# A four-layer decoder: attentions 0 and 3 in whole steps of two chunks, with three banks of scores

## The chip, the cores and the metric

The kernel runs on one core of one Trainium2 chip. The metric is the device time of one launch in microseconds (us), lower being better; the figure that counts is the median of several runs. TensorE is PE in the profile (PEld is its weight load), VectorE is DVE, ScalarE is ACT, GpSimd is POOL, and SyncE (SP) only issues transfers.

## The reference

`x` is (8, 256, 128): eight batches of 256 tokens. A context `ctx_512` is (8, 1601, 64). Four layers follow each other, each a cross-attention of `x` on the context and then a feed-forward block, all with residuals. This change concerns the attentions of layers 0 and 3, which have the same form, 16 heads of 8 channels:

```python
qh = (layernorm(x) @ Wq + bq)   # -> 16 heads x 8 channels, scaled by 8 ** -0.5
kh, vh = ctx @ Wk + bk, ctx @ Wv + bv
attn = softmax(qh @ kh.T)       # (8 batches, 16 heads, 256, 1601)
x = x + (attn @ vh).reshape(8, 256, 128) @ Wo + bo
```

(Layer 3 has no biases.) The attentions of layers 1 and 2 and the four feed-forward blocks are computed by other code.

## The kernel before

Both attentions run through the function `narrow`. The work is cut into 32 **units**: unit `n` is batch `b = n // 4` and a group `i = n % 4` of four heads. The keys and queries of a unit lie in two tiles each (`t` = 0, 1), and each tile holds two heads, one on its partitions 0 to 63 and one on 64 to 127 (`g` = 0, 1). Every value is split into a high and a low half, so a head of 8 channels fills up to 64 rows. The two heads of a tile are multiplied by two matmuls of 64 rows that lie in the two halves of the array and can run side by side.

The 1601 keys are 13 **chunks** of 128 (the last has 65). For each unit there are three kinds of work:

- **Scores** (`score`, L1069): keys stationary, queries moving, so the scores stand transposed, keys on partitions. One call treats a pair of chunks of one tile: four matmuls of 256 columns into two PSUM banks (tile `st`), one bank for each head. ScalarE takes the exponential of each bank (L1072) into the tile `e`, of which there are two in turn; one `e` holds four heads by two chunks.
- **Values** (`values`, L1081): for one chunk, four matmuls of 32 columns side by side, one for each head, accumulated over the chunks in one bank (`ov`). The operands are plain float32 and each matmul is recorded as two passes, so a chunk shows as eight. At a unit's end ScalarE copies the bank out (L1085).
- **Maxima** (`pair`, L873 and L876): the softmax needs each query's largest score beforehand. Two units ahead, the same scores are computed the other way round (queries stationary, 512 keys moving) and VectorE takes the maximum of each bank. A unit has 14 such pairs of matmuls: 12 with 512 keys, and for each tile one with the last 66 keys of both query blocks (four small matmuls). `shift` then puts the maxima together, and `place_shift` (L895) transposes them and writes them into spare rows of the queries by a transfer.

Besides, smaller steps for later batches are spread over the units from a list `beside` with due times between 0 and 1: loads of keys and queries into a ring of four (`place`, POOL's and SP's queues), the projections (`make_q`, `make_k` L777, `make_v` L834, in attention 0 also the transposes of the context L761), the output projection (L913), and in the last units steps of the feed-forward block that follows. All of those that use TensorE take a bank from the same ring as the scores (`bank()`).

The order on every engine is that of the program text (`manual_schedule`). Units take seven **steps** `p` of two chunks (the seventh has one), and each step is two **half steps** `t`. A half step issues the scores of tile `t`, then the values of one chunk of the step before, then what is due of `beside`, then what is due of `tasks`, where the pairs of maxima stand: one for each half step in the steady state, shifted by `DONE` = 8 half steps against the unit. The eight banks are three for the maxima (tag `m`, one bank a buffer), four for scores and side steps (`s`) and one for the values (`o`). A tile is allocated from its ring in turn, and the first matmul into it waits until the last reader of the tile that had the buffer before is done.

Of the kernel before, what the change touches and what calls it, by code (L numbers as in the profile page):

```python
# [33 lines left out]
F32 = mybir.dt.float32  # L34
F32R = mybir.dt.float32r
AF = mybir.ActivationFunctionType
ALU = mybir.AluOpType
AX = mybir.AxisListType

P = 128  # L40
# [9 lines left out]
TAKEN = -3.0e38  # L50
KW = LK + 1
RING = 4
DONE = 8
AFTER = 26


# [1 line left out]
def decoder_kernel(ctx: ExitStack, tc: tile.TileContext, a: dict, out: bass.AP):  # L58
    nc = tc.nc
# [7 lines left out]
    ps = {}  # L67
    big = {}

    @contextmanager  # L70
    def psum(**bufs):
        with ExitStack() as es:
            for n, k in bufs.items():
                ps[n] = es.enter_context(tc.tile_pool(name=f"ps_{n}", bufs=k, space=PS))
            yield
            ps.clear()

    def pm():
        return ps["m"].tile([P, 512], F32, tag="m", name="pm")
# [594 lines left out]
    def narrow(wq, wkT, wvT, wo, bq, bk, bv, bo, first, after=None, last=None):  # L674
# [8 lines left out]
        with ExitStack() as es:  # L683
            one = es.enter_context(tc.tile_pool(name="na1", bufs=1))
            two = es.enter_context(tc.tile_pool(name="na2", bufs=2))
            es.enter_context(psum(m=3, s=4, o=1))
            es.enter_context(tc.manual_schedule())

            def bank():
# [43 lines left out]
            def spare(n):  # L733

                pt = ps["o"].tile([P, LQ], F32, tag="o", name="ov")
                for _ in range(n):
                    nc.tensor.matmul(pt, lhsT=wkh, rhs=K[0][0][:, 0:LQ], start=True, stop=True)
# [124 lines left out]
            def maxima(n):  # L862

                mx = two.tile([P, QT, 4, 4], F32, tag="mx", name="mx", bufs=3)
                last = KW - 1536

                def pair(t, js, at, w):
                    k, q = K[n % RING][t], Q[n % RING][t]
                    pt = [pm() for g in range(2)]
                    for x, j in enumerate(js):  # L870
                        for g in range(2):
                            r = slice(64 * g, 64 * g + 64)
                            nc.tensor.matmul(pt[g][:, x * w:(x + 1) * w], lhsT=q[r, j * P:(j + 1) * P],  # L873
                                             rhs=k[r, at:at + w], start=True, stop=True)
                    for g in range(2):
                        nc.vector.tensor_reduce(mx[:, js[0]:js[-1] + 1, 2 * t + g, at // 512],  # L876
                                                pt[g][:, 0:len(js) * w].rearrange("p (j k) -> p j k", k=w),
                                                AX.X, ALU.max)

                def shift():  # L880
                    m = two.tile([P, QT, 4], F32, tag="mxn", name="mxn")
                    nc.vector.tensor_reduce(m, mx, AX.X, ALU.max, negate=True)
                    mq = M[n % 2].rearrange("p j (h s) -> p j h s", s=8)
                    nc.vector.tensor_copy(mq[:, :, :, 0], m)
                    nc.vector.tensor_tensor(mq[:, :, :, 1], m, mq[:, :, :, 0].bitcast(F32), ALU.subtract)

                order = [(j, at) for at in (0, 512, 1024) for j in range(QT)]
                return [f for t in range(2) for f in
                        (*(lambda j=j, t=t, at=at: pair(t, (j,), at, 512) for j, at in order),
                         lambda t=t: pair(t, range(QT), 1536, last))], shift  # L890
# [130 lines left out]
            for n in range(units):  # L1021
                b, i = divmod(n, 4)
                v = V[b % 2]
                if n + 2 < units:
                    plan(n + 2)

                beside = []
                if n + 3 < units:
                    beside += [((0.0, 0.25)[t], lambda t=t: place(n + 3, t)) for t in range(2)]
                beside.append((0.3, lambda: load_later(3)))  # L1030
                if n + 1 < units:
                    beside.append(((DONE + 1) / per, lambda: place_shift(n + 1)))
                if b + 1 < NB and i == 0:
                    beside += zip((0.0, 0.2, 0.5, 0.65, 0.8, 1.0),
                                  (lambda: turn_y(b + 1), lambda: make_q(b + 1), *make_k(b + 1)))
                if b + 1 < NB and i == 1:
                    beside += zip((0.2, 0.4, 0.6, 0.8), make_v(b + 1))
                if b and i == 2:
                    beside += zip((0.2, 0.35, 0.6), finish(b - 1))
                if b + 2 < NB and i == 2:  # L1040
                    load_ct(b + 2)
                    if first:
                        cuts, turns = make_ct(b + 2)
                        beside += zip((0.0, 0.0, 0.4, 0.6), cuts)
                        beside += zip((0.3, 0.5, 0.7, 0.9), turns)
                if b + 3 < NB and i == 3:
                    beside.append((0.0, lambda: load_raw(b + 3)))
                if b + 2 < NB and i == 3:
                    beside.append((0.5, lambda: (make_y(b + 2), add_bias(b + 2))))
                if after is not None and n >= AFTER:  # L1050
                    if n == AFTER:
                        late = after(left(), bank)
                    beside += [((x - per * (n - AFTER)) / per, lambda x=x: run([late[x]], EARLY + LATE))
                               for x in late if x // per == n - AFTER]
                beside.sort(key=lambda x: x[0])
                if i == 0:
                    od[b] = two.tile([P, LQ], F32, tag="od", name="od")
                    sums[b] = two.tile([P, LQ], F32, tag="sums", name="sums")
                cell = {}

                def score(p, t, e):
                    k, q = K[n % RING][t], Q[n % RING][t]
                    cs = range(2 * p, min(2 * p + 2, NC))
                    m = P if cs[-1] < NC - 1 else LAST
                    st = [bank().rearrange("p (j q) -> p j q", q=LQ) for g in range(2)]
                    for j, c in enumerate(cs):
                        for g in range(2):
                            r = slice(64 * g, 64 * g + 64)
                            nc.tensor.matmul(st[g][0:m, j, :], lhsT=k[r, c * P:c * P + m], rhs=q[r, :],  # L1069
                                             start=True, stop=True)  # L1070
                    for g in range(2):
                        nc.scalar.activation(e[0:m, 2 * t + g, 0:len(cs), :], st[g][0:m, 0:len(cs), :], AF.Exp)  # L1072

                def values(c, e, cell=cell, i=i, v=v, b=b):
                    if c == 0:
                        cell["o"] = ps["o"].tile([P, LQ], F32, tag="o", name="ov")
                    m = P if c < NC - 1 else LAST
                    for g in range(4):
                        h = 4 * i + g
                        at = 2 * D * c + 32 * (h // 2) + 2 * (h % 2)  # L1080
                        nc.tensor.matmul(cell["o"][32 * g:32 * g + 32, :], lhsT=v[0:m, at:at + 32],  # L1081
                                         rhs=e[0:m, g, c % 2, :], start=(c == 0), stop=(c == NC - 1))
                    if c == NC - 1:
                        os = two.tile([P, LQ], F32, tag="os", name="os")
                        nc.scalar.copy(os, cell["o"])  # L1085
                        at = slice(32 * i, 32 * i + 32)
                        nc.sync.dma_start(out=od[b][at, :], in_=os[0:P:4, :])
                        nc.sync.dma_start(out=sums[b][at, :], in_=os[1:P:4, :])

                for p in range(steps):  # L1090
                    e = two.tile([P, 4, 2, LQ], F32, tag="e", name="e")
                    for t in range(2):
                        score(p, t, e)
                        if n == p == 0:
                            spare(6)
                        if before:
                            before.pop(0)()
                        while beside and (beside[0][0] * 2 * steps < 2 * p + t + 1 or p * t == steps - 1):
                            beside.pop(0)[1]()
                        for f in tasks.pop(per * n + 2 * p + t, []):  # L1100
                            f()
                    before = [lambda c=c, e=e, values=values: values(c, e)
                              for c in range(2 * p, min(2 * p + 2, NC))]
            *inverses, project = finish(NB - 1)
# [829 lines left out]
```

## Time and profile before

| what | us |
|---|---|
| median of 3 runs | 3535.34 (3530.77 to 3539.5) |
| the profiled execution: span from first to last instruction | 3529.4 |
| PE busy in the span | 3380.6 (96%) |
| DVE busy | 2580.6 (73%) |
| ACT busy | 2290.0 (65%) |
| first and last scores (L1069) of attention 0, from the span's start | 55.5 to 705.8 |
| first and last scores (L1069) of attention 3 | 2685.9 to 3317.0 |

The page gives the profiled execution's span and not a time of its own beside it; the three times are 1.4 to 10.1 us above the span, the median 5.9. A matmul's recorded duration holds the time in the pipeline, so that a busy PE may still lose time between its groups; start-to-start distances show this better. "pm", "st", "ov" are the PSUM tiles of maxima, scores and values.

### The profile page before, as it was taken

To read this page: it belongs to the slowest core of one execution; us is meant where nothing else is said; L and a number is where in the kernel's file an instruction comes from. 1 tells how busy PE (TensorE), PEld (TensorE's weight loads), DVE (VectorE), ACT (ScalarE), POOL (GpSimd) and SP (SyncE) were. 2 spreads that over 40 slices of the span, in tenths; PEclk is the share of its full clock that TensorE was granted. 3 is DMA by queue.
4 is the path that set the end of the run, shared out by engine and by line. 5 is a ranking of instruction groups with operands and counts; after the bars stand their busy time and mean duration, and the time that the engine had idled before them with its cause. 6 is when DMAs were issued, how large, how long until landed. Compare 5 with 4: busy or idle time off the path is not lost.

```text
span 3529.4 us, 75160 instructions
## 1 busy us (share of the span) xinstructions
PE 3380.6 (96%) x28453; PEld 2299.7 (65%) x28453; DVE 2580.6 (73%) x6482; ACT 2290.0 (65%) x5747; POOL 1179.4 (33%) x2105
## 2 busy tenths in 40 slices
PE   7999999989999999999999999988999999999999
PEld 4555555468787877788787878866445555555444
DVE  6888888656776767676776767675557888888665
ACT  3888887746666666667666666654224878787622
POOL 6344344624152513324151520131115333332100
PEclk8999999989999999999999999999998999999999
DMA  5544444120001001000100000021004444443100
GB/s 97 89 73 74 71 77 58 19 83 1 15 1 33 2 1 39 1 15 1 39 1 22 6 1 15 1 66 33 1 0 85 78 63 68 65 69 53 41 5 7
DMA packets 113449, 130.24 MB, mean 37 GB/s; under 512 B 67616, under 2 KB 96832, under 8 KB 112448
## 3 DMA queue, kind: packets, MB, share of 16 engines
q1 hardware_dynamic: 92352, 114.22, 18.0%
q0 software_dynamic: 20480, 10.53, 1.3%
q8 instruction: 225, 3.69, 0.4%
q10 hardware_dynamic: 256, 0.69, 0.1%
q14 instruction: 136, 1.11, 0.1%
HBM read 44.79 MB, written 11.28 MB: 16 GB/s over the span
## 4 chain that ended last, share of the span: by engine, by line
PE 81%; DVE 9%; ACT 6%; POOL 2%; issue 2%; DMA 0%; DVEq 0%; POOLq 0%; SPq 0%; ACTq 0%
PE ov L1081 13%; PE o L514 12%; PE st L467 12%; PE pm L873 11%; PE t L500 8%; PE st L1069 6%; PE gu L1740 3%; PE o L1789 3%; PE gu L1741 3%; ACT pt L502 3%; DVE ls L474 2%; DVE mx L876 2%; ACT e L488 2%; PE st L834 1%; DVE ql L444 1%
## 5 line engine op out<-in xcount | busy, mean ns | idle before, releaser
L876 DVE TENSOR_REDUCE mx<-pm 128x1 f32<-128x512 f32 (+1 forms) x1792 | 1020.3, 627 | 172.7 <-PE pm L873 168.9
L1072 ACT ACTIVATE e<-st 128x512 f32<-128x512 f32 (+1 forms) x1792 | 910.6, 566 | 210.5 <-PE st L1069 160.0
L474 DVE TENSOR_REDUCE ls<-st 128x1 f32<-128x512 f32 x1088 | 549.5, 567 | 292.3 <-PE st L467 291.2
L488 ACT ACTIVATE e<-st,ls 128x512 f32<-128x512 f32 x1088 | 634.0, 602 | 13.4 <-DVE ls L477 12.6
L502 ACT COPY pt<-t 128x512 f32<-128x512 f32 x544 | 293.6, 586 | 460.8 <-PE t L500 459.9
L1081 PE MATMUL ov<-e,V 128*32 128x256 f32 x6656 | 564.6, 392 | 0.3 <-ACT e L1072 0.3
L873 PE MATMUL pm<-K,Q 64*128 64x512 f32 (+1 forms) x2048 | 497.3, 451 | 18.6 <-DVE mx L876 15.4
L500 PE MATMUL t<-ident,e 128*128 128x128 f32 (+1 forms) x3536 | 506.5, 281 | 2.6
L514 PE MATMUL o<-pt,v 128*64 128x128 f32 (+1 forms) x7072 | 490.2, 278 | 17.0 <-DVE pt L502 13.0
L514 PEld LDWEIGHTS o<-pt,v 128*64 128x64 f32 (+1 forms) x7072 | 412.1, 137 | 88.2 <-DVE pt L502 37.2
L873 PEld LDWEIGHTS pm<-K,Q 64*128 64x128 f32 x2048 | 226.1, 187 | 325.8 <-DVE mx L876 223.3
L500 PEld LDWEIGHTS t<-ident,e 128*128 128x128 f32 (+1 forms) x3536 | 391.5, 141 | 52.4 <-ACT pt L502 30.0
L467 PE MATMUL st<-ct,qh 128*128 128x512 f32 x1088 | 406.1, 373 | 1.8 <-ACT e L488 1.8
L1069 PE MATMUL st<-Q,K 64*128 64x256 f32 (+1 forms) x3328 | 403.1, 287 | 0.1
L467 PE MATMUL st<-ct,ql 128*128 128x512 f32 x1088 | 362.9, 367 | 0.0
L1069 PEld LDWEIGHTS st<-Q,K 64*128 64x128 f32 (+1 forms) x3328 | 333.1, 182 | 32.3 <-issue 6.5
L855 POOL DMA_DIRECT2D Q<-qh x256 | 128.3, 501 | 450.5 <-PE st L1069 422.9
L502 DVE COPY pt<-t 128x512 f32<-128x512 f32 (+1 forms) x544 | 239.1, 481 | 34.9 <-PE t L500 34.8
L467 PEld LDWEIGHTS st<-ct,qh 128*128 128x128 f32 x1088 | 205.6, 189 | 86.3 <-issue 34.9
L1081 PEld LDWEIGHTS ov<-e,V 128*32 128x32 f32 x6656 | 142.5, 108 | 153.7 <-issue 37.9
L1742 ACT ACTIVATE act<-gu 128x512 f32<-128x512 f32 x130 | 77.5, 597 | 243.2 <-PE gu L1741 232.1
L488 ACT ACTIVATION_READ_ACCUMULATOR e<-st,ls 128x1 f32 x1088 | 230.7, 212 | 0.0
(545 smaller groups left out, 4302.2 us busy)
## 6 DMA issues: line engine op xcount, KB each, us to landing
K<-kh SPq DMA_DIRECT2D x250, 100.1 KB
K<-kl SPq DMA_DIRECT2D x250, 100.1 KB
ct<-ctd SPq DMA_DIRECT2D x23, 801.0 KB
ctd<-ct SPq DMA_DIRECT2D x8, 801.0 KB
v<-in_ctx SPq DMA_DIRECT2D x16, 384.0 KB
Q<-qh POOLq DMA_DIRECT2D x256, 16.0 KB, 2.7
Q<-ql POOLq DMA_DIRECT2D x256, 16.0 KB, 3.0
raw<-in_ctx SPq DMA_DIRECT2D x8, 384.0 KB
```

The source lines that it names most:

```text
L467: nc.tensor.matmul(st[n, c][:, 0:w], lhsT=q[k, h][i][:, j * P:(j + 1) * P], rhs=ct[k][:, at:at + w], start=(i == 0), stop=(i == 1))
L474: nc.vector.tensor_reduce(ls[n][:, c:c + 1], st[n, c][:, 0:BANK[c][1]], AX.X, ALU.max)
L488: nc.scalar.activation(e[n][:, at:at + w], st[n, c][:, 0:w], AF.Exp, bias=ls[n][:, 4:5], scale=1.0, accum_out=ls[n][:, 5 + c:6 + c])
L500: nc.tensor.transpose(t[0:m, (c - 4 * i) * P:(c - 4 * i + 1) * P], e[n][:, c * P:c * P + m], ident)
L502: (nc.scalar.copy if i < 2 else nc.vector.tensor_copy)(p[0:m, 0:w], t[0:m, 0:w])
L514: nc.tensor.matmul(o[n][half, 0:P], lhsT=v[k][0:m, c, :], rhs=turned[n, c // 4][0:m, (c % 4) * P:(c % 4 + 1) * P], start=(c < 2), stop=(c ...
L855: nc.gpsimd.dma_start(out=q[r:P:8, :].bitcast(F32), in_=qhl[b][r % 2][src, :].bitcast(F32))
L873: nc.tensor.matmul(pt[g][:, x * w:(x + 1) * w], lhsT=q[r, j * P:(j + 1) * P], rhs=k[r, at:at + w], start=True, stop=True)
L876: nc.vector.tensor_reduce(mx[:, js[0]:js[-1] + 1, 2 * t + g, at // 512], pt[g][:, 0:len(js) * w].rearrange("p (j k) -> p j k", k=w), AX.X, ...
L1069: nc.tensor.matmul(st[g][0:m, j, :], lhsT=k[r, c * P:c * P + m], rhs=q[r, :], start=True, stop=True)
L1072: nc.scalar.activation(e[0:m, 2 * t + g, 0:len(cs), :], st[g][0:m, 0:len(cs), :], AF.Exp)
L1081: nc.tensor.matmul(cell["o"][32 * g:32 * g + 32, :], lhsT=v[0:m, at:at + 32], rhs=e[0:m, g, c % 2, :], start=(c == 0), stop=(c == NC - 1))
```

## The change

In `narrow` alone (both attentions): a pair of maxima is one tile of two banks with one reduction instead of two; the maxima have two such tiles (four banks), scores and side steps have three banks instead of four. A step is no longer two half steps: it issues the scores of tile 0, then the pairs of maxima due in both half steps, then the scores of tile 1, then what is due of `beside`, then the values of both chunks of the step before. `DONE` is 6 instead of 8.

```diff
-DONE = 8
+DONE = 6
...
-            es.enter_context(psum(m=3, s=4, o=1))
+            es.enter_context(psum(mm=2, s=3, o=1))
...
                 def pair(t, js, at, w):
                     k, q = K[n % RING][t], Q[n % RING][t]
-                    pt = [pm() for g in range(2)]
+                    pt = ps["mm"].tile([P, 2, 512], F32, tag="mm", name="pm")
                     for x, j in enumerate(js):
                         for g in range(2):
                             r = slice(64 * g, 64 * g + 64)
-                            nc.tensor.matmul(pt[g][:, x * w:(x + 1) * w], lhsT=q[r, j * P:(j + 1) * P],
+                            nc.tensor.matmul(pt[:, g, x * w:(x + 1) * w], lhsT=q[r, j * P:(j + 1) * P],
                                              rhs=k[r, at:at + w], start=True, stop=True)
-                    for g in range(2):
-                        nc.vector.tensor_reduce(mx[:, js[0]:js[-1] + 1, 2 * t + g, at // 512],
-                                                pt[g][:, 0:len(js) * w].rearrange("p (j k) -> p j k", k=w),
+                    to = mx[:, js[0]:js[-1] + 1, 2 * t:2 * t + 2, at // 512]
+                    if len(js) == 1:
+                        nc.vector.tensor_reduce(to[:, 0, :], pt[:, :, 0:w], AX.X, ALU.max)
+                    else:
+                        nc.vector.tensor_reduce(to.rearrange("p j g -> p g j"),
+                                                pt[:, :, 0:len(js) * w].rearrange("p g (j k) -> p g j k", k=w),
                                                 AX.X, ALU.max)
...
                 for p in range(steps):
                     e = two.tile([P, 4, 2, LQ], F32, tag="e", name="e")
+                    score(p, 0, e)
+                    if n == p == 0:
+                        spare(6)
                     for t in range(2):
-                        score(p, t, e)
-                        if n == p == 0:
-                            spare(6)
-                        if before:
-                            before.pop(0)()
-                        while beside and (beside[0][0] * 2 * steps < 2 * p + t + 1 or p * t == steps - 1):
-                            beside.pop(0)[1]()
                         for f in tasks.pop(per * n + 2 * p + t, []):
                             f()
+                    score(p, 1, e)
+                    if n == p == 0:
+                        spare(6)
+                    while beside and (beside[0][0] * 2 * steps < 2 * p + 2 or p == steps - 1):
+                        beside.pop(0)[1]()
+                    for f in before:
+                        f()
                     before = [lambda c=c, e=e, values=values: values(c, e)
                               for c in range(2 * p, min(2 * p + 2, NC))]
```

## The prediction

> **What bounds the kernel now.** First the page's engines and chain, for which engine sets the end.
>
> ```profile
> PE 3380.6 (96%) x28453; PEld 2299.7 (65%) x28453; DVE 2580.6 (73%) x6482; ACT 2290.0 (65%) x5747; POOL 1179.4 (33%) x2105
> PE 81%; DVE 9%; ACT 6%; POOL 2%; issue 2%; DMA 0%; DVEq 0%; POOLq 0%; SPq 0%; ACTq 0%
> ```
>
> PE carries the end. The table by stretches for 24 steady units of attention 3 (us, then busy time of PE, PEld, DVE, ACT, POOL; granted clock) and the waits there:
>
> ```profile
> 2780.00:3253.00 473.00, 471.56 (x4822) 258.44 (x4820) 408.42 (x764) 378.33 (x780) 172.12 (x321) 1.00 0.43 65
> PEld pm L873 <- DVE mx L876: 76.0, 187, 0.6
> ```
>
> DVE is 86% busy and ACT 80%, at full clock. PE seems busy throughout, but its groups have gaps that show in the timeline only (start, length). One step from 2997.64 on, then ACT in it:
>
> ```profile
> 2997.64 0.54 PE L873 MATMUL pm<-K,Q 64*128 64x512 f32 x2
> 2997.98 0.44 PE L1069 MATMUL st<-Q,K 64*128 64x256 f32 x4
> 2998.35 0.64 PE L1081 MATMUL ov<-e,V 128*32 128x256 f32 x8
> 2998.92 0.50 PE L873 MATMUL pm<-K,Q 64*128 64x512 f32 x2
> 2999.26 0.40 PE L1069 MATMUL st<-Q,K 64*128 64x256 f32 x4
> 2999.59 0.64 PE L1081 MATMUL ov<-e,V 128*32 128x256 f32 x8
> 3000.16 0.45 PE L873 MATMUL pm<-K,Q 64*128 64x66 f32 x4
> 3000.40 0.53 PE L1069 MATMUL st<-Q,K 64*128 64x256 f32 x4
> 3000.98 1.09 ACT L1072 ACTIVATE e<-st 128x512 f32<-128x512 f32 x2 [0.20 <-PE st L1069]
> ```
>
> A half step is pm, st, ov: 1.28 and 1.24, a step 2.52; over the steady half steps of both stages the medians give 2.51. Between starts of single matmuls in the trace: pm to st 0.34; first to second pair of st 0.12; st to ov 0.21; one pass of a chunk's values to the next 0.24; ov to what follows 0.33. Streaming 512 columns takes 0.21 (256-column groups follow at 0.11 at best), so the two changes of array layout in a half step, row halves to column quarters and back, cost some 0.33: 0.10 and 0.09 of draining, and the first weight load after a change, 0.11, stands in the open (pm to st is 0.23 where that load was early, 0.34 here; two st pairs after a change stand 0.22 apart, not 0.12). The 0.04 by which alternate half steps differ is the DVE wait above: pm's second matmul needs the bank of the reduction before.
>
> A unit's length, read from the copy at its end, without side steps but `place_shift`: 17.78.
>
> ```profile
> 2991.93 0.38 ACT L1085 COPY os<-ov 128x256 f32<-128x256 f32 x1
> 3009.71 0.38 ACT L1085 COPY os<-ov 128x256 f32<-128x256 f32 x1
> ```
>
> With side steps, units of attention 3 take 20.8, 21.1 and 19.2.
>
> **The change, part by part.** The build order of the changed kernel shows the step as st, pm, pm, st, side steps, ov, ov, and each wait's partner.
>
> *Layout changes.* Four a step become two: if nothing waited, a step would be, from its first st: 0.22 to the second pair, 0.12 to pm, 0.23 to the second pm, 0.23 to st, 0.12, 0.21 to ov, three times 0.24, 0.33 to the next: 2.18. Against 2.51 this saves 0.33 a step.
>
> *Maxima.* DVE's 128x512 reductions last 684 ns and start 608 apart, the 128x132 ones last 289: 1.04 ns an element. So 128x1024 lasts about 1.22 and the next can start after 1.14; 24 become 12 and DVE's unit falls by 12 x (1.216 - 1.14) = 0.9 us. DVE isn't the bound, so this is nothing by itself. Two tiles for two pairs a step bind so: the second pair waits for the second reduction of the step before, 0.41 + 1.14 + 1.22 + 0.05 = 2.82 after that step's first pm; with 1.90 of PE work behind it two steps take 4.72, so DVE's loop allows 2.36 a step.
> The Trainium skill (Perfetto Trace Analysis, Optimizing Scalar/DVE Operations) gives a DVE operation on PSUM about 125 ns of fixed cost, where the rows leave 608 - 512 x 1.04 = 76 ns; by its figure the merge would save 1.5 us of DVE a unit, off PE's path all the same. The same section says that where these engines aren't saturated but cause bubbles on others, breaking instructions up may let work finish sooner: that speaks against this change, which makes them longer.
>
> *Three banks of scores.* This decides. A `score` call takes two banks, so the second call's second bank is the one that the first call's first head filled in the same step. By the build order, its matmul waits for that head's exponential; PE is strictly in order, and queued behind it are the side steps, both chunks of values and the next scores, for which then ACT and DVE wait. From the step's start:
> - second pair of st: 0.22;
> - exponential starts 0.37 later (3000.61 to 3000.98; 0.31 where it waits for PE alone, but a step's first also waits for an older ACT instruction, as now): 0.59;
> - it lasts 0.598 (mean of that shape): 1.19; a load starts 0.05 after the end that frees it (peak in the trace for pm after DVE): 1.24. PE has been ready since 0.80: 0.44 lost;
> - second pair 0.22 later, its load being late: 1.47; ov 1.68; three passes: 2.40; next step 2.73.
> So a full step goes from 2.51 to 2.73: the 0.33 saved against 0.44 of wait and 0.11 of load that is no longer hidden. Both DVE's 2.36 and ACT's four exponentials (0.495 apart, 2.0) fit below it, and the DVE wait on pm disappears into it.
> The Trainium skill (Perfetto Trace Analysis, Optimization Strategy) takes a gap that repeats on the engine to be saturated as a sign that PSUM is short for the next tile; before, no such gap shows on st, and the sum above expects one.
>
> *A unit.* Step 0 has one chunk of values: 2.73 - 0.48 = 2.25. Five full: 13.65. The last (65 keys, exponential 0.376): 2.10. `place_shift` behind the second scores waits for the second head's bank (free at 1.73), then 0.12 + 0.21: 0.38. The copy of `ov` stands ahead of a first exponential: 0.10. Together 18.5 against 17.78: +0.7. (Before holds a wait of 0.42 a unit for exponentials at the first values, which goes.)
>
> *Side steps.* Each now stands 0.26 after the scores and 0.21 before ov, in place of 0.31 and 0.21 less the 0.35 of ov to pm: +0.1. One that follows the short `place_shift` waits for the third bank until 2.32: +0.26. For each four units attention 0 has 15 and 3 of these, attention 3 has 11 and 1: +0.57 and +0.34 a unit. Their ACT copies find ACT free (2.66 of a step of 3.1 and more).
>
> *Queues.* `place` moves by under a half step: K's eight transfers on SP and Q's ten on POOL a unit keep 6 half steps or more until use; POOL waits for st only because the ring's slot must be free, and this has that slack too. `place_shift` goes from half step 9 to the end of step 3, three steps (8.2 us) ahead of use, with a landing of about 3 (the page's Q loads): nothing; uncovered, a few us a unit.
>
> *Ends.* In unit 31 and half of unit 30 there are no maxima. A step there was twice 0.43 + 0.57 = 2.0 and becomes 2.73:
>
> ```profile
> 3298.60 0.50 PE L1069 MATMUL st<-Q,K 64*128 64x256 f32 x4
> 3299.03 0.64 PE L1081 MATMUL ov<-e,V 128*32 128x256 f32 x8
> ```
>
> Unit 31 took 15.5 in attention 3 and would take 18.0; with unit 30, +5.5 for each attention. At the start, 14 pairs fall on three steps instead of four and are bound by DVE either way: 0, within 2.
>
> *Sum.* Units 1 to 25: 25 x (0.7 + 0.57) + 25 x (0.7 + 0.34) = 58. Units 26 to 29, with feed-forward steps, at 1.3: 8 x 1.3 = 10. Ends: 11. Together +79 on the span of 3529.4: 3608; with the 5.9 between span and median, **3614 us**. The unsure terms: the 0.37 could be 0.31 and the passes of two chunks could follow at 0.21, 0.12 less a step, 7 x 57 x 0.12 = 48 less: 3566. Above, if every feed-forward side step and half of the others wait for a third bank (0.26): 8 x 8 x 0.26 + 160 x 0.13 = +37: 3651.
>
> **Rivals.**
> 1. *The wait on the three banks is hidden, and DVE's loop is the bound.* Then a step is 2.36, step 0 is 1.88, the last 1.96, the unit 16.1: 1.7 less, 64 x 1.7 = 109, about 3426. This needs the exponential of the first bank to be over when PE arrives, at 0.80 instead of 1.24; the change breaks even with before where the loop is shorter by about 0.2. For it: DVE and ACT have room. Against: the row of 3000.98 and the mean of 598 leave no place for 0.2.
> 2. *Side steps pay more.* With three banks, two or three side steps in a row each wait for an exponential, and DVE's reductions of 1.22 delay what else DVE does (`shift`, the output's sum). At twice the side terms above: +40, 3655; point of decision: st's first bank of a step waiting for a side step.
> 3. *The steps cancel* (loop at 2.6, side steps free): within 0.3%.
>
> **How the numbers follow.** About 0.3%, 11 us, is what this measurement can tell from no change. Forecast 3566 to 3640: 0.70; rival 2, above: 0.12; rival 3: 0.06, of which 0.05 within 0.3%, the rest slower; rival 1, and mixtures with it that are faster: 0.12. So faster 0.12, same 0.05, slower 0.83. The range 3540 to 3670 leaves out rival 1, the lower half of rival 3 and the far end of rival 2, less than 0.2.
>
> **What would show it.** Right: in a steady step, st's second call starts some 1.2 after the first, PE idle 0.4 before it, released by ACT's exponential; a step of 2.7, 64*128 weight loads of st with about 0.4 x 380 = 150 us of idle time released by `e`; 128x1024 reductions of about 1.2 us; a unit without side steps of 18.5. Wrong: units shorter than 17.8; pm's second load waiting for DVE as the main wait; the second st call following pm at 0.23; reductions well over 1.3 us.

## The result, and the profile after

The changed kernel takes 3596.09 us (median of 4 runs, 3592.98 to 3601.52) against 3537.42 (4 runs, 3530.77 to 3544.26) for the kernel before on the same chip: a ratio of 1.0167, interval 1.0147 to 1.0186. It is slower; the forecast was 3614. The profiled execution took 3592.98 with a span of 3591.3, which is 61.9 more than before. In the code after, pm is at L873, its reductions at L877 and L879, scores at L1072, exponentials at L1075, values at L1084, the copy of `ov` at L1088, `place_shift` at L898, `make_k` at L777 and `make_v` at L834.

The page's engines and the chain of waits that ended last:

```profile
PE 3354.6 (93%) x28453; PEld 2321.9 (65%) x28453; DVE 2512.4 (70%) x5586; ACT 2288.7 (64%) x5747; POOL 1176.7 (33%) x2105
PE 72%; ACT 11%; DVE 10%; issue 3%; POOL 3%; DMA 1%; SPq 0%; POOLq 0%; ACTq 0%; DVEq 0%
```

DVE did 68 us less work and the kernel became 62 longer. PE's share of the chain fell from 81% to 72%, and ACT's rose from 6% to 11%: PE now waits for ACT. The list of waits over the span names the wait (us, times, longest), and the group of merged reductions (busy, mean ns) has the forecast length:

```profile
PEld st L1072 <- ACT e L1075: 246.5, 551, 2.0
```

```profile
L877 DVE TENSOR_REDUCE mx<-pm 128x2 f32<-128x1024 f32 x768 | 907.5, 1220 | 265.6 <-PE pm L873 261.5
```

The timeline of one full step without side steps, from 3049.73 to 3052.40 (start, length):

```profile
3049.73 0.50 PE L1072 MATMUL st<-Q,K 64*128 64x256 f32 x4
3050.07 0.62 PE L873 MATMUL pm<-K,Q 64*128 64x512 f32 x4
3050.52 0.28 PE L1072 MATMUL st<-Q,K 64*128 64x256 f32 x1
3050.97 0.50 PE L1072 MATMUL st<-Q,K 64*128 64x256 f32 x3 [0.17 <-ACT e L1075]
3051.40 1.07 PE L1084 MATMUL ov<-e,V 128*32 128x256 f32 x16
3052.40 0.50 PE L1072 MATMUL st<-Q,K 64*128 64x256 f32 x4
```

```profile
3050.32 2.16 ACT L1075 ACTIVATE e<-st 128x512 f32<-128x512 f32 x4 [0.66 <-PE st L1072]
```

The second call's first score goes into the free third bank at 3050.52. Its second bank is free only when the first exponential, begun at 3050.32, is over: the other three start at 3050.97, 1.24 after the step's start, which is the figure that the prediction worked out. The two pm groups between them no longer wait for DVE.

The units by the copies at their ends (attention 3; the last gap, 18.43, ends a unit whose only side step is `place_shift`; before, 17.78), and in PE the first scores of that unit and of the next:

```profile
3022.66 0.38 ACT L1088 COPY os<-ov 128x256 f32<-128x256 f32 x1
3041.61 0.38 ACT L1088 COPY os<-ov 128x256 f32<-128x256 f32 x1
3060.04 0.41 ACT L1088 COPY os<-ov 128x256 f32<-128x256 f32 x1
```

```profile
3038.96 0.50 PE L1072 MATMUL st<-Q,K 64*128 64x256 f32 x4
3057.14 0.51 PE L1072 MATMUL st<-Q,K 64*128 64x256 f32 x4
3058.97 0.41 PE L808 MATMUL st<-ident,ln_y 128*128 128x128 f32 x2
3059.32 0.64 PE L1084 MATMUL ov<-e,V 65*32 65x256 f32 x8
```

The gap of 18.43 is too long for a unit's length: the next unit's first side step (L808) now stands ahead of the last values, and so ahead of the copy; before, it stood behind them. From first score to first score that unit takes 18.18, and 17.78 before. Lengths of a bare unit (`place_shift` its only side step) are counted so from here on; the recorded expectations still count by the copies.

Cut at these copies, the 61.9 us are:

| stretch | attention 0 | attention 3 |
|---|---|---|
| first score to the end of unit 0 | 30.4 to 39.8, +9.4 | 30.5 to 39.8, +9.3 |
| units 1 to 25 | 500.4 to 520.9, +20.5 | 492.9 to 507.4, +14.5 |
| units 26 to 31 | 122.2 to 127.9, +5.7 | 109.4 to 113.6, +4.2 |

Everything outside the two attentions adds up to -1.7. The +18.7 at the two starts was not forecast. There the 14 pairs of maxima due in unit 0 stand in groups of five, five and four between two scores calls, and the timeline of attention 3's start and the table by stretches (42 us from there; clock in the third column from the end) show this:

```profile
2721.57 0.49 PE L873 MATMUL pm<-K,Q 64*128 64x512 f32 x2 [1.10 <-DVE mx L877]
2722.71 0.50 PE L873 MATMUL pm<-K,Q 64*128 64x512 f32 x2 [0.64 <-DVE mx L877]
2723.84 0.80 PE L873 MATMUL pm<-K,Q 64*128 64x512 f32 x2 [0.63 <-DVE mx L877]
2733.30 1.94 PE L1084 MATMUL ov<-e,V 128*32 128x256 f32 x16
```

```profile
2718.00:2760.00 42.00, 35.17 (x260) 20.17 (x260) 27.50 (x30) 21.88 (x44) 17.44 (x30) 0.80 0.29 54
```

With two tiles a pair follows each 1.13, the time after which the next reduction can start, and PE stands before each. The granted clock is 0.80 over these 42 us, and PE runs at about half speed for a while: sixteen value passes take 1.94 here and 1.07 in the step above.

### The profile page after: what moved, and what is told of

The parts are those of the page before. It is cut to its first block, busy times and chain, and to the rows that moved or that the text cites. A ratio compares the mean times of both kernels' runs of the same rounds, so it can differ in the third digit from the quotient of the medians.

```text
span 3591.3 us, 74415 instructions
## 1 busy us (share of the span) xinstructions
PE 3354.6 (93%) x28453; PEld 2321.9 (65%) x28453; DVE 2512.4 (70%) x5586; ACT 2288.7 (64%) x5747; POOL 1176.7 (33%) x2105
## 3 DMA queue, kind: packets, MB, share of 16 engines
q1 hardware_dynamic: 92352, 114.22, 18.5%
## 4 chain that ended last, share of the span: by engine, by line
PE 72%; ACT 11%; DVE 10%; issue 3%; POOL 3%; DMA 1%; SPq 0%; POOLq 0%; ACTq 0%; DVEq 0%
PE o L514 12%; PE st L467 11%; PE ov L1084 10%; PE st L1072 9%; PE t L500 8%; ACT e L1075 5%; DVE mx L877 4%; PE gu L1746 3%; PE gu L1747 3%; PE o L1795 3%; ACT pt L502 3%; PE pm L873 2%; DVE ls L474 2%; PE st L834 2%; ACT e L488 2%
## 5 line engine op out<-in xcount | busy, mean ns | idle before, releaser
L1075 ACT ACTIVATE e<-st 128x512 f32<-128x512 f32 (+1 forms) x1792 | 913.5, 565 | 303.8 <-PE st L1072 296.4
L877 DVE TENSOR_REDUCE mx<-pm 128x2 f32<-128x1024 f32 x768 | 907.5, 1220 | 265.6 <-PE pm L873 261.5
L1072 PE MATMUL st<-Q,K 64*128 64x256 f32 (+1 forms) x3328 | 535.1, 332 | 62.8 <-ACT e L1075 56.0
L1072 PEld LDWEIGHTS st<-Q,K 64*128 64x128 f32 (+1 forms) x3328 | 330.9, 183 | 370.3 <-ACT e L1075 246.5
L514 PE MATMUL o<-pt,v 128*64 128x128 f32 (+1 forms) x7072 | 492.9, 279 | 16.9 <-DVE pt L502 13.0
L1084 PE MATMUL ov<-e,V 128*32 128x256 f32 x6656 | 457.2, 389 | 0.0
L873 PE MATMUL pm<-K,Q 64*128 64x512 f32 (+1 forms) x2048 | 320.5, 380 | 31.1 <-DVE mx L877 20.5
L1084 PEld LDWEIGHTS ov<-e,V 128*32 128x32 f32 x6656 | 171.9, 109 | 143.3 <-issue 42.3
L467 PEld LDWEIGHTS st<-ct,ql 128*128 128x128 f32 x1088 | 206.0, 189 | 37.0
```

The costliest lines, as they stand in the source:

```text
L467: nc.tensor.matmul(st[n, c][:, 0:w], lhsT=q[k, h][i][:, j * P:(j + 1) * P], rhs=ct[k][:, at:at + w], start=(i == 0), stop=(i == 1))
L514: nc.tensor.matmul(o[n][half, 0:P], lhsT=v[k][0:m, c, :], rhs=turned[n, c // 4][0:m, (c % 4) * P:(c % 4 + 1) * P], start=(c < 2), stop=(c ...
L873: nc.tensor.matmul(pt[:, g, x * w:(x + 1) * w], lhsT=q[r, j * P:(j + 1) * P], rhs=k[r, at:at + w], start=True, stop=True)
L877: nc.vector.tensor_reduce(to[:, 0, :], pt[:, :, 0:w], AX.X, ALU.max)
```

## The experiments

The theory is that the whole-step order costs its time where the second scores wait for the step's first exponential, plus a part at the start. Rivals: the banks and the long reductions cost it; side steps cost it; ScalarE as a whole does; at the start, the clock alone does. Times below are medians, with the ratio to the kernel before (run again beside each batch, 3540.7 to 3542.0) and its 95% interval; segments come from one profiled execution of each kernel. The edits are shown against the changed kernel, in experiment 5 against experiment 4 and in experiment 9 against experiment 1.

### 1. New banks and merged maxima, old order

```diff
-DONE = 6
+DONE = 8
...
-                    score(p, 0, e)
-                    if n == p == 0:
-                        spare(6)
                     for t in range(2):
+                        score(p, t, e)
+                        if n == p == 0:
+                            spare(6)
+                        if before:
+                            before.pop(0)()
+                        while beside and (beside[0][0] * 2 * steps < 2 * p + t + 1 or p * t == steps - 1):
+                            beside.pop(0)[1]()
                         for f in tasks.pop(per * n + 2 * p + t, []):
                             f()
-                    score(p, 1, e)
-                    if n == p == 0:
-                        spare(6)
-                    while beside and (beside[0][0] * 2 * steps < 2 * p + 2 or p == steps - 1):
-                        beside.pop(0)[1]()
-                    for f in before:
-                        f()
```

> The half-step order and DONE = 8 of before, with the changed kernel's pools and merged reductions (maxima in two two-bank tiles, three banks of scores). Theory (the loss is the wait of a step's second scores for the first head's exponential, because whole steps put the two score calls 0.8 us apart): in half steps the calls stand 1.23 us apart and the bank is free after some 1.1, so there is no wait; the wait of pm for DVE goes too, the half step is 1.23 instead of 1.23 and 1.28, unit 0 isn't burst at half clock, and the unit without side steps takes about 17.5 us; the time is about 3515 us, faster than before. Rival (three banks or the 1.22 us reductions cost by themselves): slower than before here too, 3560 or more.

Measured: 3520.24, ratio 0.9945 (0.9924 to 0.9965), so faster than the kernel before, as expected. Unit 0 takes 27.3 (30.4 before), a bare unit 17.68, units 1 to 25 take 497.2 and 487.0. The banks and the merged reductions together are a gain of some 20 us by the ratio; what costs on these banks is the order with its `DONE`, 76 us between the medians of this kernel and the changed one.

### 2. The first call's two exponentials swapped

```diff
-                    for g in range(2):
+                    for g in ((1, 0) if t == 0 else (0, 1)):
                         nc.scalar.activation(e[0:m, 2 * t + g, 0:len(cs), :], st[g][0:m, 0:len(cs), :], AF.Exp)
```

> The changed kernel with the two exponentials of a step's first score call in the other order, nothing added. The bank that the second call needs is then free 0.495 us later. Theory: each of the five to six full steps of a unit grows from 2.67 to about 3.17 us, 57 to 64 units by 2.5 to 3 us: 3740 to 3790 us. Rival (DVE's loop of 2.36 us a step, or PE's own 2.2, with the wait only shown where another one would stand): up to 0.2 us a step, under 3670 us.

Measured: 3602.72 (1.0174, 1.0137 to 1.0212), no different from the changed kernel. The expectation was wrong about the buffers, and so was the kernel's description above ("in turn"): as the wait shows, a new tile got the buffer that comes free first in program order. The second scores waited again for whichever exponential ran first (it ended at 3022.017, the scores went on at 3022.070). The wait had not been varied, so this says nothing about the theory.

### 3. The first exponential twice

The dose the other way, with values unchanged:

```diff
-                        nc.scalar.activation(e[0:m, 2 * t + g, 0:len(cs), :], st[g][0:m, 0:len(cs), :], AF.Exp)
+                        for _ in range(2 if g == t == 0 and len(cs) == 2 else 1):
+                            nc.scalar.activation(e[0:m, 2 * t + g, 0:len(cs), :], st[g][0:m, 0:len(cs), :], AF.Exp)
```

> The first exponential of every full step is issued twice in a row, on the same bank with the same result; nothing else is changed. ScalarE starts its exponentials 0.495 apart, so that bank comes free 0.495 later. Theory (the second bank of the second scores waits for the first exponential of its step): the wait of 0.45 grows by 0.45 to 0.5 in each of a unit's six full steps, a clean full step 2.67 becomes 3.12 to 3.17, a unit without side steps 18.4 becomes 21.0 to 21.5, and the time grows by 64 x 6 x 0.45 to 0.5, to 3755 to 3790. Rival (the wait is not for this exponential): ScalarE has about 0.7 to spare in a step of 2.67, so nothing is paid: 3590 to 3610.

Measured: 3898.25 (1.1015, 1.0978 to 1.1053). A full step in the timeline, PE and then ACT:

```profile
3087.95 0.50 PE L1072 MATMUL st<-Q,K 64*128 64x256 f32 x4
3088.29 0.54 PE L873 MATMUL pm<-K,Q 64*128 64x512 f32 x6
3088.66 0.36 PE L1072 MATMUL st<-Q,K 64*128 64x256 f32 x1
3089.76 0.50 PE L1072 MATMUL st<-Q,K 64*128 64x256 f32 x3 [0.74 <-ACT e L1076]
3090.20 1.07 PE L1085 MATMUL ov<-e,V 128*32 128x256 f32 x16
```

```profile
3088.48 2.80 ACT L1076 ACTIVATE e<-st 128x512 f32<-128x512 f32 x5 [0.87 <-PE st L1072]
```

The other three scores now start 1.81 after the step instead of 1.24, and a step is 3.25 instead of 2.67: +0.58 for some 0.6 of hold, while ScalarE has idle time before each step. This settles the wait. The dose was missed in two ways. The repeat started 0.63 after the first, not 0.495, and PE at these longer waits lost its clock in places:

```profile
2840.00:3320.00 480.00, 392.16 (x3626) 228.45 (x3626) 310.73 (x380) 345.89 (x688) 164.79 (x291) 0.90 0.40 58
```

Sixty-four units at 3.5 more (a bare unit went from 18.18 to 21.70) are 225 of the 302; the clock, 0.90 here and 1.00 in the changed kernel over the same stretch, goes with the rest, which was not split further.

### 4. A shorter first exponential, and the rest taken from the second bank

The first exponential covers the first head's first chunk only; a third one, out of the second head's bank, fills the slice that is left. The values of that slice are not the softmax's.

```diff
+                        nj = 1 if g == t == 0 else len(cs)
-                        nc.scalar.activation(e[0:m, 2 * t + g, 0:len(cs), :], st[g][0:m, 0:len(cs), :], AF.Exp)
+                        nc.scalar.activation(e[0:m, 2 * t + g, 0:nj, :], st[g][0:m, 0:nj, :], AF.Exp)
+                    if t == 0 and len(cs) == 2:
+                        nc.scalar.activation(e[0:m, 0, 1:2, :], st[1][0:m, 1:2, :], AF.Exp)
```

> The changed kernel with the first bank released earlier: the first exponential of a step treats one chunk (256 columns) of the first head, and the second chunk of that head takes its exponential from the second head's bank, so that ACT's work stays; the softmax of one head in four is therefore not the reference's. The first exponential lasts about 0.376 instead of 0.598 us. Theory: the wait of 0.45 us shrinks by 0.22, a full step goes from 2.67 to 2.45 us, above DVE's 2.36; 57 units by 5 to 6 steps by 0.22: 3520 to 3535 us. Rival (DVE's reductions set the step): no gain beyond 20 us.

Measured: 3591.95 (1.0146, 1.0125 to 1.0167): a miss in the total, though a clean full step did fall from 2.67 to 2.47, with the first exponential at 0.38 instead of 0.60. The third exponential holds the second bank longer, and who needs that bank is the side step:

```profile
3024.13 0.40 PE L898 MATMUL st<-ident,M 128*32 128x128 f32 x2 [0.27 <-ACT e L1078]
```

L1078 is the added exponential. A step with `place_shift` took 3.12 (3.06 in the changed kernel), one with `make_v` 3.84 (3.78). The edit had moved the wait to the other bank. The total holds one thing more: in the profiled execution unit 31 of attention 3 ran at a granted clock of 0.53 and took 23.8 instead of 16.5.

### 5. The same without the hold

```diff
-                        nc.scalar.activation(e[0:m, 0, 1:2, :], st[1][0:m, 1:2, :], AF.Exp)
+                        nc.scalar.copy(e[0:m, 0, 1:2, :], e[0:m, 1, 1:2, :])
```

> The first exponential of a full step reads only the first head's first chunk (0.384 long in the run with a third exponential, instead of 0.598); the slice it leaves out is filled by a copy on ScalarE inside SBUF from the second head's result, so that no score bank is held for it. The values of one slice are not the softmax's. Theory (the whole-step order loses its time to the bank that the first exponential holds): a clean full step 2.47 as in that run, and now steps with a side step and the first step of a unit keep the 0.2 too, since no third exponential holds the second bank: unit without side steps 17.2 to 17.6, time 3515 to 3545. Rival (the loss is ScalarE's total in a step, which the added copy does not lower): as with the third exponential, unit 17.97 or more, 3585 to 3600.

Measured: 3554.9 (1.0043, 1.0029 to 1.0058); 10 us above the range expected, but 41 below the changed kernel, at the cost of a copy on ScalarE in each step (ScalarE busy 400 of 480 us in the steady stretch, 374 in the changed kernel). A clean step is 2.41, one with `place_shift` 2.79, a bare unit 17.27, and units 1 to 25 take 500.9 and 486.3: 41 less than in the changed kernel, and 6 less than before. So a shorter hold of one bank takes back the whole loss of the steady units, although ScalarE works more. What is left against the kernel before is the start, still 39.3 and 39.2 (+17.7).

### 6. Side steps inside the wait

```diff
+                    while beside and (beside[0][0] * 2 * steps < 2 * p + 2 or p == steps - 1):
+                        beside.pop(0)[1]()
                     score(p, 1, e)
...
-                    while beside and (beside[0][0] * 2 * steps < 2 * p + 2 or p == steps - 1):
-                        beside.pop(0)[1]()
                     for f in before:
                         f()
```

> The side steps of a step (place_shift, make_k, make_v, project, cuts) go between the pairs of maxima and the second scores instead of behind the second scores; nothing else is changed. Theory (the second scores wait 0.27 to 0.45 for the first exponential, with no other work in front of them): the side steps then fill that wait, a step with place_shift falls from 3.07 to about 2.83, a unit without side steps (one place_shift in it) from 18.43 to about 18.2, units with make_k or make_v by about 1; some 100 to 170 side steps at 0.24 to 0.45: 3540 to 3565. Rival (the wait is for something else in front of the second scores, or a side step ends its own pass later): 3590 to 3600.

Measured: 3573.24 (1.0102, 1.0082 to 1.0123): a gain of 23, half of the one expected. Steps with `make_k` fell from 3.40 to 3.17 and with a whole `make_v` from 3.78 to 3.38 (medians; single ones between 3.28 and 3.86), but one with `place_shift` rose from 3.06 to 3.17, a bare unit with it from 18.18 to 18.28, and one with the short last `make_v` from 3.00 to 3.16. A side step takes a score bank too, and in front of the second scores it takes the free third one; the second scores then wait for both exponentials. A step with that short `make_v`:

```profile
2999.64 0.22 PE L834 MATMUL st<-wvl,ct 128*65 128x128 f32 x1
2999.87 0.99 PE L1072 MATMUL st<-Q,K 64*128 64x256 f32 x4
```

Those four matmuls take 0.99 with the wait for the second exponential inside, against 0.50 for the first call's. Only steps that are long enough to cover both waits gain.

### 7. The whole-step order with the old banks

```diff
-            es.enter_context(psum(mm=2, s=3, o=1))
+            es.enter_context(psum(m=3, s=4, o=1))
...
-                    pt = ps["mm"].tile([P, 2, 512], F32, tag="mm", name="pm")
+                    pt = [pm() for g in range(2)]
...
-                    to = mx[:, js[0]:js[-1] + 1, 2 * t:2 * t + 2, at // 512]
...
+                    for g in range(2):
+                        nc.vector.tensor_reduce(mx[:, js[0]:js[-1] + 1, 2 * t + g, at // 512],
+                                                pt[g][:, 0:len(js) * w].rearrange("p (j k) -> p j k", k=w),
```

> The whole-step order with DONE = 6, but with the pools of before (three one-bank tiles for maxima, four banks of scores) and one reduction per bank. Theory (order alone): no wait for the first exponential on four banks of scores, but the four banks of maxima of a step come on three, so the second pair waits for VectorE: its reductions take 0.608 each (start to start), 2.43 a step, and the second pair's last bank waits for the first reduction (about 0.6 to 0.75 after its matmul): a full step 2.7 to 3.1, time 3600 to 3720. Rival (the order costs nothing with enough banks of scores): step 2.3 to 2.45, 3440 to 3520.

Measured: 3815.7 (1.0779, 1.0758 to 1.0799), above the range. The four banks of scores leave no wait in the clean step, but four banks of maxima come on three:

```profile
3029.54 0.51 PE L1069 MATMUL st<-Q,K 64*128 64x256 f32 x4
3029.88 0.62 PE L873 MATMUL pm<-K,Q 64*128 64x512 f32 x3
3031.06 0.50 PE L873 MATMUL pm<-K,Q 64*128 64x512 f32 x1 [0.55 <-DVE mx L876]
3032.72 0.33 PE L1069 MATMUL st<-Q,K 64*65 64x256 f32 x2
```

The fourth matmul starts 1.52 after the step, and the step is 3.18. The expectation of 2.7 to 3.1 was near; beyond it unit 0 takes 44.5 and 44.4 (30.4 and 30.5 before), and the clock fell, to 0.91 over 2840 to 3320. With this order the same kind of wait appears on whichever side has the fewer banks: four of scores and four of maxima would leave out both, and with the values' bank that is nine of eight.

### 8. The start: DONE, the clock, the order

> The changed kernel with DONE = 8 as before. In unit 0 the 14 pairs of maxima then fall on four steps instead of three. Theory on the start (five pairs in a row wait for DVE with nothing else in PE's queue, the granted clock falls to half, and unit 0 takes 39.8 instead of 30.4 us): with three to four pairs a step PE's share rises, unit 0 takes 34 us or less in both attentions and the time is about 3585 us; steady units stay at 18.4. Rival (the start is bound by DVE's 14 reductions alone): unit 0 stays within 2 us of 39.8 and the time within 5 of 3596.

(The edit is `DONE = 8` alone.) Measured: 3578.06 (1.0112, 1.0084 to 1.0139); unit 0 takes 34.7 and 34.5 instead of 39.8, close to the 34 expected, and the rival is out; a bare unit stays at 18.18. So 10.4 of the 18.7 at the starts come with `DONE` = 6, the clock included: over unit 0 it is 0.90 here and 0.79 in the changed kernel, and this run doesn't separate the two.

Spare matmuls between the pairs of the first unit:

```diff
                         for f in tasks.pop(per * n + 2 * p + t, []):
                             f()
+                            if n == 0 and p < 2:
+                                spare(4)
```

> Four spare matmuls after each of the pairs of maxima in the first two steps of unit 0 of each attention, where TensorE waits about 1.1 between the pairs and the trace shows passes 0.43 apart (half the clock) in the stretches behind it. Theory (the waiting TensorE lost its clock there): with the spare matmuls granted clock stays near 1.00 in the first unit, unit 0 falls from 39.8 to 34 to 37 in both attentions, 3585 to 3590 in all. Rival (unit 0 is long because of the tail of 14 pairs behind VectorE alone): unit 0 39 to 41, 3596 to 3600.

Measured: 3602.5 (1.0182, 1.0163 to 1.0201), no gain. In attention 0 the granted clock over 53 to 93 went from 0.79 to 1.00, and unit 0 fell only from 39.8 to 36.9; in attention 3 the first two groups of pairs ran at full speed too, the third, which has no spare matmuls, was followed by value passes of 1.93, and the unit took 39.1. The clock is thus some 3 of the 9.4; with PE at full clock the pairs stay 1.10 apart. The spare matmuls, up to 0.74 a group, may themselves cost a little, which would make the clock's share larger. The total says nothing on this: in the profiled execution the two units 31, which the edit doesn't touch, took 27.8 and 23.7 (25.9 and 16.5 in the changed kernel) at clocks of 0.69 and 0.57.

The old interleaving in the first unit alone, DONE at 6:

```diff
                     for t in range(2):
+                        if n == 0 and t == 1:
+                            score(p, 1, e)
+                            if p == 0:
+                                spare(6)
+                        if n == 0 and before:
+                            before.pop(0)()
                         for f in tasks.pop(per * n + 2 * p + t, []):
                             f()
-                    score(p, 1, e)
-                    if n == p == 0:
-                        spare(6)
+                    if n > 0:
+                        score(p, 1, e)
```

> The changed kernel with the first unit of each attention in the old interleaving (a pass of values and one of two task slots behind each scores call), all other units in whole steps; DONE stays 6. Theory (the start of each attention is long because the pairs of maxima of the first unit stand together between two scores calls, on two tiles): unit 0 falls from 39.8 to 31 to 34 in both, time 3580 to 3587. Rival (the start is long because DONE = 6 leaves less room for the 14 pairs): unit 0 37 or more, 3592 to 3600.

Measured: 3582.92 (1.0138, 1.0103 to 1.0173); unit 0 takes 32.0 and 32.7, 7.8 and 7.1 less, and the clock in these stretches is 1.00 and 0.96. The total agrees with that but its interval reaches that of the changed kernel, so the segments carry the verdict. Either change, more room before the maxima are due or scores and values between the pairs, takes back more than half of the 18.7, and both bring the clock up as well.

### 9. A further step on the faster kernel

The kernel of experiment 1 waits some 0.4 once a unit for exponentials, behind the copy of `ov`. Here the maxima of that half step come before the values:

```diff
+                        if p == 1 and t == 0:
+                            for f in tasks.pop(per * n + 2 * p + t, []):
+                                f()
                         if before:
                             before.pop(0)()
```

> On the half-step kernel with the new pools and merged maxima (the faster one): in the second step of a unit the first pair of maxima stands ahead of the values as well as the scores, so that the values (which wait some 0.4 there for the exponentials behind the copy of the unit's output) come later. Theory: TensorE waits less there, 0.2 in a unit, 3505 to 3512. Rival (the wait returns at the next step, or the scores come later by what is put in front of them): 3517 to 3525.

Measured: 3518.35 (0.9946, 0.9926 to 0.9966), the same as experiment 1. A bare unit went from 17.68 to 17.63, unit 0 from 27.3 to 28.5. The rival holds. Experiments 1 and 9 are the versions that beat both kernels.

## Why the prediction was right or wrong

*The mechanism was right.* The wait, its place and its partner are as the sum had them: second scores 1.24 after the first, released by the first head's exponential; reductions of 1.22; the pm wait for DVE nearly gone (11.0 us over 2840 to 3320, where the prediction's stretch of 473 had 76.0). Experiments 3 and 5 vary this hold in both directions, and the step follows: 2.67 to 3.25, and to 2.41.

*The step, 2.73 forecast, 2.67 measured.* The difference is mostly a term marked as unsure: the passes of two chunks in a row follow at 0.24, 0.216 and 0.216. A bare unit was given 18.5, +0.7, and took 18.18, +0.40; five full steps at 0.06 less are the 0.3. The forecast of about 150 us of waiting for `e` counted 380 waits of 0.4; the trace has 551 at 0.45 on average, 246.5.

*The unit and the side steps were mis-sized.* Units 1 to 25 were given +58 and took +35.0. The bare units are 20 of this (50 at 0.40) where 35 were given, and the side steps 15 where +0.57 and +0.34 a unit summed to 23. By kind of unit, in the steady state, from first score to first score and beyond the 0.40 (given: by the terms of +0.1 and +0.26):

| side steps of the unit | given | measured |
|---|---|---|
| projections of queries and keys | 0.86 | 0.75 |
| the four `make_v` | 0.4 | 0.28 |
| output projection, attention 0 (with transposes) | 1.0 | 0.7 |
| output projection, attention 3 | 0.1 | -0.65 |

So the terms were somewhat large throughout, and one has the other sign: what was left out is that before, side steps also brought waits which now vanish. It shows in the trace before, in a unit of attention 3 that went from 19.18 to 18.94: DVE's reciprocals for the output held up the reductions, and pm on its one-bank tiles stood behind them. From the step's first exponential to the next step's that is 3.19; it is 2.68 now, as for a clean step.

```profile
2977.76 0.94 DVE L907 RECIPROCAL rs<-sums 128x128 f32<-128x128 f32 x1
2978.56 0.49 PE L873 MATMUL pm<-K,Q 64*128 64x512 f32 x1
2979.30 0.49 PE L873 MATMUL pm<-K,Q 64*128 64x512 f32 x1 [0.24 <-DVE mx L876]
```

The sum looked only at the clean steps of before for what goes. Why the other terms came out smaller was not measured.

*The ends* (units 26 to 31) took +9.9 of +21 forecast. In attention 3, units 30 and 31 took +3.3 and +1.0, of +5.5. In attention 0, unit 31 took 25.9 against 21.0, but at a granted clock of 0.80 where it was 1.00 before. In the whole-step kernels that kept 1.00 there (experiments 2, 6, 7 and the last of 8) it took between 19.9 and 22.2, and with the clock at 0.69 (the first two of 8) 27.8. So most of its +4.9 goes with the clock, and the forecast for the ends was too large by more than the sum shows.

*The start was wrong.* It was put at "0, within 2", on the ground that the pairs are bound by DVE either way. The trace of before had the clue: its four steps held scores and values between the pairs, which then ran beside the reductions. Grouped in three steps, PE can only wait between pairs, and the scores and values come afterwards. It cost 18.7, a term that the sum had at nothing. The two errors, -34 for units 1 to 31 and +18.7 for the start, partly cancel. That the total came within 18 of the forecast is luck to this extent: without the cost of the start it would have been some 37 below.

*The rivals.* DVE's loop of 2.36 is not the bound while the hold is there; with the hold shortened, the clean step comes to 2.41 and `pm L873 <- DVE mx L877` returns among the waits (25.0 us over 2840 to 3320, 11.0 in the changed kernel). The rival that side steps pay twice is refuted: twice the side terms would have been +45 in units 1 to 25, and the side steps took 15. The layout changes saved pay a little in a clean step (2.41 in experiment 5, 2.47 for two half steps in experiment 1), but experiment 5 with 987.2 for units 1 to 25 is no faster there than experiment 1 with 984.2, which has four layout changes a step: a bare unit gains 0.4 against it, and the units with projections of queries and keys or of the output lose 0.3 to 1.0.

## What to carry to other kernels

Count PSUM banks against the program order: when a group of work takes N banks twice and the ring has fewer than 2N, the second group waits for the evacuation (the reading out by another engine) of the first, unless that is over by then, and everything behind it on an engine that works in program order waits too. The price is the evacuation's end minus the work in between, and here it could be read off the trace beforehand (0.44 forecast, 0.45 on average measured). Look at the start and end of a pipeline by themselves: grouping work that used to be interleaved costs most where no steady state covers it, and count also the waits that a change removes around side steps.

## What the runs showed of the hardware

The granted clock fell without any long pause. In experiment 3 two scores stand 1.0 to 1.15 apart once a step with PE waiting between them. After one such 1.15, from 3109.79 on, sixteen value passes took 1.94, about half speed; after another, from 3137.35 on, they took 1.07 as usual. The clock over 2840 to 3320 was 0.90. With 0.45 between them, in the changed kernel, it stayed at 1.00 over the same stretch. The Trainium skill (TensorE: Matmul & The Clock Gate, Why this matters for your kernels) advises to avoid idle gaps over about 3 us; the pauses here were well below that, and the measurement decides. Which pauses bring the clock down no run here shows. The same page (A second HAM failure mode: psum-queue depth-cycling) describes short idling between groups that cycle through PSUM banks and a clock that goes back and forth, which agrees with these rows.

A repeated exponential on the same bank and into the same place starts 0.63 after the first instead of 0.495: the second does not overlap the first's end.
